# Neighbour sums of a two-layer GNN: four tiles of a slot in one burst, one-hots two slots ahead, and a gather ring that borrows the place of weights

## Chip, cores and metric

The kernel runs on one core of a Trainium2 chip. The metric is the device time of one execution in microseconds, as the median of several runs. A profile is one further execution, recorded by the hardware profiler.

## What is computed

The input `x` has 6250 nodes of 512 values, and there are 100,000 edges `src -> dst`, sorted by `dst`. Two mean-aggregating graph layers run on the normalised nodes, their result is added to `x`, and a mixture of eight experts with the best two per node is added to that.

```python
def _sage_layer(h, src, dst, W_self, W_neigh, b, n_nodes):
    agg = segment_sum(h[src], dst)
    deg = segment_sum(ones_like(dst), dst)
    h_neigh = agg / maximum(deg, 1.0)[:, None]
    return relu(h @ W_self + h_neigh @ W_neigh + b)
...
def _moe_forward(x, Wg, W1, b1, W2, b2, gamma, beta):
    topv, topi = top_k(xf @ Wg, 2)
    gate_w = softmax(topv)
    h = relu(einsum('td,edh->teh', xf, W1) + b1)
    y = layernorm(einsum('teh,ehd->ted', h, W2) + b2) * gamma + beta
    return sum(gate_w * take_along_axis(y, topi))
...
x = x + two _sage_layers(layernorm(x))
x = x + _moe_forward(layernorm(x))
```

All arithmetic on the rows is in float32.

## The kernel before

**Blocks, tiles, slots.** The nodes are cut into NB = 49 blocks of 128. The edges are cut into 782 tiles of 128. The row of each edge's source node is fetched from HBM by an indirect DMA that POOL issues (`gather`, L214), one per tile: 128 rows of 2 KB. A group is NQ x TS = 12 tiles, worked in TS = 3 slots of NQ = 4 tiles, so there are about 196 slots in a layer. For each slot DVE builds a one-hot table `hot` (`build`, L224), which says to which of 32 consecutive nodes an edge belongs. PE multiplies it with the gathered rows (`add`, L244): four tiles go to four column strips of 32 of PE's array and to the four quarters of one PSUM bank, `pa`. A matmul of float32 appears as two passes in the trace. After three slots `close` copies `pa` to SBUF (ACT, L252). When the groups that can hold a block's edges are closed, `prepare` builds selection matrices `sel` (DVE, L269), and `take_out` adds the strips up for the block (PE, L278). That happens every third slot, or, for 16 of the blocks, after six.

**What runs in the slots.** `sums` is called once for each layer. It writes the program of PE, DVE, ACT and POOL by hand, in the order of its loop. Within slot `i` the order was: `gather(i + ahead)`, then `build(i + 1)`, the sums of tiles 0 and 1, whatever is due in the place "mid", the sums of tiles 2 and 3, `close`, and whatever is due in the place "post". An engine executes its instructions in that order. The instructions of SP's queue are ordered by the compiler's scheduler.

What is due comes from `finish`, called by `take_out`:

- First layer (`layer1`): transposes u1 in "mid" two slots later, copied out of PSUM by ACT (L190), and the projection u2 on them in "post" of the same slot (L386); transposes u3 and projection u4 in the slot after; u5 in the next. For blocks from 19 on, u0 is one more projection.
- Second layer (`route`): DVE and ACT make the block's own result and its normalised rows `xn` (L833 to L839); then `turn` (transposes, "mid", slot 2), `logits` ("post", slot 2), `experts` ("mid", 3: a small transpose, then DVE chooses two experts), `rank` ("mid", 4: two small matmuls, then DVE counts places), `send` ("mid", 5 and 6: an indirect DMA of POOL scatters the rows to `xs`, L823) and `share` ("post", 6).
- Also in the second layer, from the time when the first lists of rows are known, `each` begins in every even slot the first expert product of one 128-row tile (an "up"): its rows are fetched by SP (L698), transposed by `turn_x` in "mid" three slots later, multiplied with W1 in `times` ("post" of that slot, L709), and turned by `turn_h` one slot later (L717, L720). These products are kept in HBM (`hd`).

After the second layer a last stage computes the remaining ups, the down products with W2 (L969), and the combination.

**Buffers.** The gathered rows of the first layer lie in 16 tiles, `rows_t`, of 256 KB, fetched three slots ahead. Those of the second layer lie in a ring of 12 such places in the tile `big`, behind W1, fetched two slots ahead (`ring`). W2 lies in the tile `w2`, 8 MB, loaded by SP with one DMA of 1 MB for each expert (`load_w2`, L455), asked for in `route` of blocks 1, 7, 13 and so on to 43. In SP's compiled order all eight stand at the start of the second layer. `xn` has two places, for even and odd blocks. `apart` is a memset of one element on POOL (L535), issued ahead of the scatters of the last four blocks.

Of the kernel before, what the change touches and what calls it, by code (L numbers as in the profile page):

```python
# [67 lines left out]
def gnn_moe(ctx, tc, x, src, dst, Ws1, Wn1, gb1, Ws2, Wn2, gb2, Wg, W1, b1, W2, b2, gamma, beta, out):  # L68
# [122 lines left out]
        return tT  # L191


    def sums(z, pool, pap, room, pn, finish, ring, nring, each=None):

        nslot = (NG - 1) * TS + min(TS, NT_E - (NG - 1) * NQ * TS)  # L200
        ahead = nring // NQ - 1
        tiles = [[t for t in range(i // TS * NQ * TS + i % TS, min(NT_E, (i // TS + 1) * NQ * TS), TS)]
                 for i in range(nslot)]
        gathered, hots, few, strips, counts, sels, due = {}, {}, {}, {}, {}, {}, {}
# [5 lines left out]
        def gather(i):  # L210
            if i < nslot:
                for t in tiles[i]:
                    gathered[t] = ring()
                    nc.gpsimd.indirect_dma_start(  # L214
                        out=gathered[t], out_offset=None, in_=z[:, :],
                        in_offset=bass.IndirectOffsetOnAxis(ap=srcT[:, t : t + 1], axis=0))
# [17 lines left out]
                nc.vector.tensor_add(few[g][:, :m], before[:, :m], hots[i][:, :m])  # L234
                few[g, j] = few[g]

        def add(i, qs):
            g, j = divmod(i, TS)
            if pa[0] is None:
                pa[0] = pap.tile([P, D], F32, name="pa", bufs=2)  # L240
            for q in qs:
                if q < len(tiles[i]):
                    t = tiles[i][q]
                    nc.tensor.matmul(pa[0][q * SW : (q + 1) * SW], hots[i][:, q], gathered.pop(t), start=(j == 0),  # L244
                                     stop=(j == TS - 1 or t == NT_E - 1), tile_position=(0, q * SW))

        def close(i):

# [32 lines left out]
            for behind, place, what in finish(b, ps) if pn is None else finish(b, ps, pn[:, 1]):  # L281
                at(i + behind, place, what)

        for i in range(ahead):
            gather(i)
        build(0)
        i = 0
        while i < nslot or any(k[0] >= i for k in due):
            gather(i + ahead)
            if each is not None:  # L290
                for behind, place, what in each(i):
                    at(i + behind, place, what)
            build(i + 1)
            if i < nslot:
                add(i, (0, 1))
            for what in due.pop((i, "mid"), ()):
                what()
            if i < nslot:
                add(i, (2, 3))
                if i % TS == TS - 1 or i == nslot - 1:  # L300
                    close(i)
            for what in due.pop((i, "post"), ()):
                what()
            i += 1
# [7 lines left out]
    def part(i):  # L312
        return big[:, i * D : (i + 1) * D]
# [61 lines left out]
    with tc.tile_pool(name="s1", bufs=2, side="right") as pool, \  # L375
            tc.tile_pool(name="s1a", bufs=1, space=PSUM) as pap, \
            tc.tile_pool(name="s1p", bufs=2, space=PSUM) as psp:

        def layer1(b, pa, pd):
            n = rows[b]  # L380
            r = slice(b * P, b * P + n)
            own = {}

            def project(ph, tT, w, start, stop):
                for c in range(C):
                    nc.tensor.matmul(ph, tT[:, c], w[:, c], start=(start and c == 0), stop=(stop and c == C - 1))  # L386

            def u0():
                ps = psp.tile([P, D], F32, name="pm")
                project(ps, xnT[b], ws1, True, True)  # L390
                nc.vector.tensor_add(part(b), ps, bb1)

            def u1():
                own["aT"] = transposed(pool, psp, own["a"], AF.Copy)

            def u2():
                ph = psp.tile([P, D], F32, name="pm")
                project(ph, own["aT"], wn1, True, True)
                own["h"] = pool.tile([P, D], F32, name="h")
                nc.vector.tensor_add(own["h"], ph, part(b))  # L400

            def u3():
                own["hT"] = transposed(pool, psp, own["h"], AF.Relu)

            def u4():
                pz = psp.tile([P, D], F32, name="pm")
                project(pz, own["hT"], wn2, True, True)
                t = pool.tile([P, D], F32, name="z")
                nc.scalar.copy(t, pz)
                nc.sync.dma_start(z2[r], t[:n])  # L410

            def u5():
                ps = psp.tile([P, D], F32, name="pm")
                project(ps, own["hT"], ws2, True, True)
                t = pool.tile([P, D], F32, name="s")
                nc.vector.tensor_add(t, ps, bb2)  # L416
                nc.sync.dma_start(s2[r], t[:n])

            nc.vector.tensor_copy(deg[:, b : b + 1], pd[:, 0:1])  # L419
            nc.vector.tensor_scalar(rcnt[:, b : b + 1], deg[:, b : b + 1], 1.0, None, op0=OP.max)  # L420
            nc.vector.reciprocal(rcnt[:, b : b + 1], rcnt[:, b : b + 1])
            own["a"] = pool.tile([P, D], F32, name="a")
            nc.scalar.activation(own["a"], pa, AF.Copy, scale=rcnt[:, b : b + 1])
            e = (b - 5) // 4
            if b >= 5 and (b - 5) % 4 == 0 and e < NE:

                nc.sync.dma_start(w1[:, e * KD : (e + 1) * KD].rearrange("p (c h) -> p c h", c=C),
                                  W1[e].rearrange("(c p) h -> p c h", p=P))
            return ([] if b < NS else [(1, "post", u0)]) + [(2, "mid", u1), (2, "post", u2), (3, "mid", u3), (3, "post", u4), (4, "post", u5)]

        with tc.manual_schedule(engines=HAND):
            sums(xn_d, pool, pap, lambda: pap.tile([P, D], F32, name="ps"),
                 pap.tile([P, 2, NDEG], F32, name="pn"), layer1,
                 lambda: pool.tile([P, D], F32, name="rows_t", bufs=16), 16)
    b_ctx.close()


# [298 lines left out]
    with tc.tile_pool(name="s2", bufs=2, side="right") as pool, \  # L736
# [3 lines left out]
        own = {}  # L740
        ready = {}
        at_slot = [0]
        nring = [0]

        bet = part(NW + 16)[:NE]
        nc.sync.dma_start(bet, beta)

        def ring():
            nring[0] += 1
            return part(NW + (nring[0] - 1) % 12)  # L750

        def fetch_own(b):
            if b < NB:
# [7 lines left out]
        def route(b, pa):  # L761
# [56 lines left out]
                nc.sync.dma_start(accs[r], acc[:n])  # L818

            def send(k):  # L820
                if b >= NB - 4:
                    apart()
                inst = nc.gpsimd.indirect_dma_start(  # L823
                    out=xs[:, :], out_offset=bass.IndirectOffsetOnAxis(ap=slot[:n, b, k : k + 1], axis=0),
                    in_=t["xn"][:n], in_offset=None)
                free_of(inst, "xs")
# [5 lines left out]

            nc.vector.scalar_tensor_tensor(a[:n], pa[:n], rcnt[:n, b : b + 1], a[:n], op0=OP.mult, op1=OP.add)  # L833
            nc.vector.scalar_tensor_tensor(acc[:n], a[:n], 0.0, acc[:n], op0=OP.max, op1=OP.add)
            if b % 6 == 1 and b // 6 < NE:
                load_w2(b // 6)
            mv, rs = norm_stats(pool, acc[:n], n)
            t["xn"] = part(NW + 13 + b % 2)
            nc.vector.tensor_scalar(t["xn"][:n], acc[:n], mv[:n, 0:1], rs[:n], op0=OP.subtract, op1=OP.mult)  # L839
# [20 lines left out]

        fetch_own(0)
        with tc.manual_schedule(engines=HAND):
            sums(z2, pool, pap, lambda: psp.tile([P, D], F32, name="ph"), None, route, ring, 12, each)
    g_ctx.close()


# [331 lines left out]
```

## Time and profile before

| | |
|---|---|
| median of 3 runs | 3282.5 us (3280.71 to 3284.29) |
| the profiled execution | 3665.66 us |
| its span | 3663.9 us |
| mean granted PE clock in it | 0.903 |
| PE busy | 3038.6 us, 83% |
| POOL busy | 1800.4 us, 49% |
| DVE busy | 1131.4 us, 31% |
| ACT busy | 659.3 us, 18% |
| moved by DMA | 698.76 MB, mean 191 GB/s |
| first sums | about 195 to 1480 us of the span |
| second sums | about 1490 to 2960 us, with ups from about 2000 |
| last stage | from about 2960 us |

A line of the timeline gives the start and the duration in us, the engine, the line of the kernel, the operation, what it writes and reads, and in brackets how long the engine was idle before and what ended that. In the groups, the numbers behind the bar are busy time, mean time of one in ns, and the idle time ahead of them with what ended it. "issue" is time in which the engine waited for nothing that the profile shows. "remote" and "another core or an unknown queue" name a release that the profile can't assign. A DMA of POOL has the time of its issue, not of its transfer.

### The profile page before, as it was taken

What the parts mean: (1) busy time and instruction counts of PE and PEld (TensorE: products, weight loads), DVE (VectorE), ACT (ScalarE), POOL (GpSimd) and SP (SyncE); (2) the same over time, 40 slices, a digit from 0 to 9 for tenths busy, and PEclk for the clock granted to TensorE, in tenths of its full rate; (3) what the DMA queues carried; (4) which work ended last, traced back from release to release, by engine and by line L of the source; (5) the groups of instructions that cost most, each with busy time, mean ns of one, the idle gap of its engine ahead of it and who ended that gap; (6) DMA issues with size and microseconds to landing.
All of it is one profiled execution on the core that took longest, in us unless ns stands there. A gap on an engine that the chain in (4) does not pass through costs nothing.

```text
span 3663.9 us, 33902 instructions
## 1 busy us (share of the span) xinstructions
PE 3038.6 (83%) x9794; PEld 1156.2 (32%) x9794; DVE 1131.4 (31%) x4001; ACT 659.3 (18%) x1188; POOL 1800.4 (49%) x1970
## 2 busy tenths in 40 slices
PE   7778888999999999466666888888888877999994
PEld 3223333333333333111111333333333333334442
DVE  5311111111111111132233333433343334443464
ACT  1211111111111111011111222222222211222221
POOL 0266555555555552466666555555555438000253
PEclk9889999999999999777777888898898988999997
DMA  6566666665666653666666766666677634441496
GB/s 241 183 186 203 199 195 200 192 185 177 185 188 176 178 171 103 239 200 208 199 204 200 214 214 215 209 217 213 214 228 218 189 105 155 135 132 61 156 308 233
DMA packets 269498, 698.76 MB, mean 191 GB/s; under 512 B 42448, under 2 KB 44090, under 8 KB 269148
## 3 DMA queue, kind: packets, MB, share of 16 engines
q0 software_dynamic: 142912, 463.42, 42.9%
q1 hardware_dynamic: 121372, 224.59, 17.9%
q10 hardware_dynamic: 5024, 8.50, 0.7%
q8 instruction: 85, 1.39, 0.2%
q14 instruction: 105, 0.86, 0.1%
HBM read 557.43 MB, written 139.71 MB: 190 GB/s over the span
## 4 chain that ended last, share of the span: by engine, by line
PE 70%; another core or an unknown queue 10%; DVE 7%; issue 6%; DMA 4%; ACT 2%; SPq 0%; DVEq 0%; POOL 0%; ACTq 0%; POOLq 0%
PE pm L386 17%; PE pa L244 15%; PE py L969 9%; PE ph L709 7%; PE ph L278 5%; PE pt L188 4%; PE ph L945 3%; PE ps L278 2%; PE ph L816 2%; PE pm L366 2%; DMA out<-acc 1%; PE small L775 1%; DMA xt<-in_x 1%; PE pt L717 1%
## 5 line engine op out<-in xcount | busy, mean ns | idle before, releaser
L214 POOL DMA_INDIRECT rows_t<-xn_d,srcT x782 | 742.1, 949 | 654.9 <-PE pa L244 262.9
L214 POOL DMA_INDIRECT big<-z,srcT x782 | 752.6, 962 | 609.3 <-issue 167.9
L244 PE MATMUL pa<-big,hot 128*32 128x512 f32 x1564 | 443.9, 684 | 107.5 <-DVE hot L224 63.0
L969 PE MATMUL py<-w,hT 128*128 x840 | 395.4, 614 | 40.4 <-DVE y L986 21.8
L244 PE MATMUL pa<-rows_t,hot 128*32 128x512 f32 x1564 | 348.5, 632 | 93.1 <-DVE hot L224 30.0
L386 PE MATMUL pm<-wn,tT 128*128 128x512 f32 x784 | 368.6, 613 | 22.0 <-ACT tT L190 21.7
L709 PE MATMUL ph<-big,xgT 128*128 x544 | 288.7, 680 | 68.7 <-ACT xgT L190 24.0
L905 POOL DMA_INDIRECT big<-ys,yrow x98 | 107.4, 1096 | 427.6 <-DMA ys<-y 331.3
L969 PEld LDWEIGHTS py<-w,hT 128*128 128x128 f32 x840 | 153.6, 193 | 219.3 <-issue 172.1
L386 PEld LDWEIGHTS pm<-wn,tT 128*128 128x128 f32 x784 | 144.9, 195 | 207.8 <-issue 163.7
L709 PEld LDWEIGHTS ph<-big,xgT 128*128 128x128 f32 x544 | 113.2, 219 | 230.5 <-issue 143.9
L386 PE MATMUL pm<-ws,tT 128*128 128x512 f32 x392 | 181.1, 605 | 0.0
L190 ACT ACTIVATE tT<-pt 128x512 f32<-128x512 f32 x117 | 69.0, 596 | 565.4 <-PE pt L188 408.7
L244 PEld LDWEIGHTS pa<-big,hot 128*32 128x32 f32 x1564 | 65.9, 114 | 247.9 <-issue 111.7
L945 PE MATMUL ph<-big,xgT 128*128 x296 | 136.9, 605 | 0.0
L823 POOL DMA_INDIRECT xs<-big,slot x98 | 98.8, 1008 | 71.6 <-DVE g L560 44.0
L419 DVE COPY deg<-pn 128x1 f32<-128x1 f32 x49 | 7.7, 158 | 408.4 <-PE pn L280 245.2
L720 DVE TENSOR_SCALAR hT<-pt,b1T 128x128 f32<-128x128 f32 x272 | 76.6, 344 | 166.4 <-PE pt L717 132.3
L976 DVE BATCH_NORM_STATS2 st<-py 128x6 f32<-128x512 f32 x105 | 73.2, 697 | 160.2 <-PE py L971 157.8
L244 PEld LDWEIGHTS pa<-rows_t,hot 128*32 128x32 f32 x1564 | 47.4, 110 | 233.5 <-issue 130.8
L416 DVE TENSOR_TENSOR s<-pm,bb 128x512 f32<-128x512 f32 x49 | 33.9, 691 | 272.0 <-PE pm L386 272.0
L224 DVE TENSOR_TENSOR hot<-rel,iota_row 128x128 f32<-128x128 bf16 (+1 forms) x394 | 106.0, 281 | 26.6 <-issue 12.4
(622 smaller groups left out, 3391.5 us busy)
## 6 DMA issues: line engine op xcount, KB each, us to landing
xg<-xs SPq DMA_DIRECT2D x105, 256.0 KB
ys<-y SPq DMA_DIRECT2D x105, 256.0 KB
hd<-hT SPq DMA_DIRECT2D x68, 256.0 KB
hT<-hd SPq DMA_DIRECT2D x68, 256.0 KB
rows_t<-xn_d,srcT POOLq DMA_INDIRECT x782
big<-z,srcT POOLq DMA_INDIRECT x782
xt<-in_x SPq DMA_DIRECT2D x12, 1024.0 KB
xn_d<-xn SPq DMA_DIRECT2D x12, 1024.0 KB
```

The source lines that it names most:

```text
L188: nc.tensor.transpose(pt[:, c, :n], t[:n, c * P : (c + 1) * P], ident[:n, :n])
L214: nc.gpsimd.indirect_dma_start(out=gathered[t], out_offset=None, in_=z[:, :], in_offset=bass.IndirectOffsetOnAxis(ap=srcT[:, t : t + 1], a ...
L224: nc.vector.tensor_tensor(hots[i][:, :m], rel.rearrange("p (c j) -> p j c", j=TS)[:, j, g * NQ : g * NQ + m] .rearrange("p (t o) -> p t o" ...
L244: nc.tensor.matmul(pa[0][q * SW : (q + 1) * SW], hots[i][:, q], gathered.pop(t), start=(j == 0), stop=(j == TS - 1 or t == NT_E - 1), tile ...
L278: nc.tensor.matmul(ps, sel[:k], st[:k], start=(g == a), stop=(g == z))
L386: nc.tensor.matmul(ph, tT[:, c], w[:, c], start=(start and c == 0), stop=(stop and c == C - 1))
L709: nc.tensor.matmul(ph, self.xT[:, c], w1[:, bass.ds(self.e * KD + c * D, D)], start=(c == 0), stop=(c == C - 1))
L720: nc.vector.tensor_scalar(hT[:, c], pt[:, c], b1T[:, bass.ds(self.e * HC + c, 1)], 0.0, op0=OP.add, op1=OP.max)
L823: inst = nc.gpsimd.indirect_dma_start(out=xs[:, :], out_offset=bass.IndirectOffsetOnAxis(ap=slot[:n, b, k : k + 1], axis=0), in_=t["xn"][: ...
L905: nc.gpsimd.indirect_dma_start(out=yk[:n], out_offset=None, in_=ys[: ready[0] * P, :], in_offset=bass.IndirectOffsetOnAxis(ap=yrow[:n, b, ...
L945: nc.tensor.matmul(ph, u.xT[:, c], w1[:, bass.ds(u.e * KD + c * D, D)], start=(c == 0), stop=(c == C - 1))
L969: nc.tensor.matmul(py, hT[:, c], w2[:, bass.ds(e * KD + c * D, D)], start=(c == 0), stop=False)
```

## The change

1. `add` sums all four tiles of a slot in one burst. What was due in "mid", between the halves, comes after the burst.
2. `build` runs two slots ahead in place of one.
3. The number of slots that a gather runs ahead becomes a function, `ahead`. In the first layer it stays 3. In the second layer `ring` has seven groups of four places for the slots before `near` = 147: three in `big` as before, and four in the half of `w2` that belongs to experts 4 to 7. The gathers then run six slots ahead. From slot 147 on it is three groups and two slots as before.
4. The loads of W2 for experts 4 to 7 are asked for in `route` of blocks 40, 42, 44 and 46. In SP's compiled order they stand behind the load of the input rows of about block 36.
5. `apart` is issued ahead of each of the 98 scatters, in place of the last eight.

```diff
@@ -191,14 +191,13 @@
         return tT
-    def sums(z, pool, pap, room, pn, finish, ring, nring, each=None):
+    def sums(z, pool, pap, room, pn, finish, ring, ahead, each=None):
-        ahead = nring // NQ - 1
         tiles = [[t for t in range(i // TS * NQ * TS + i % TS, min(NT_E, (i // TS + 1) * NQ * TS), TS)]
                  for i in range(nslot)]
         gathered, hots, few, strips, counts, sels, due = {}, {}, {}, {}, {}, {}, {}
@@ -210,7 +209,7 @@
         def gather(i):
             if i < nslot:
                 for t in tiles[i]:
-                    gathered[t] = ring()
+                    gathered[t] = ring(i, t)
                     nc.gpsimd.indirect_dma_start(
                         out=gathered[t], out_offset=None, in_=z[:, :],
                         in_offset=bass.IndirectOffsetOnAxis(ap=srcT[:, t : t + 1], axis=0))
@@ -234,15 +233,13 @@
                 nc.vector.tensor_add(few[g][:, :m], before[:, :m], hots[i][:, :m])
                 few[g, j] = few[g]
-        def add(i, qs):
+        def add(i):
             g, j = divmod(i, TS)
             if pa[0] is None:
                 pa[0] = pap.tile([P, D], F32, name="pa", bufs=2)
-            for q in qs:
-                if q < len(tiles[i]):
-                    t = tiles[i][q]
-                    nc.tensor.matmul(pa[0][q * SW : (q + 1) * SW], hots[i][:, q], gathered.pop(t), start=(j == 0),
-                                     stop=(j == TS - 1 or t == NT_E - 1), tile_position=(0, q * SW))
+            for q, t in enumerate(tiles[i]):
+                nc.tensor.matmul(pa[0][q * SW : (q + 1) * SW], hots[i][:, q], gathered.pop(t), start=(j == 0),
+                                 stop=(j == TS - 1 or t == NT_E - 1), tile_position=(0, q * SW))
         def close(i):
@@ -281,22 +278,23 @@
             for behind, place, what in finish(b, ps) if pn is None else finish(b, ps, pn[:, 1]):
                 at(i + behind, place, what)
-        for i in range(ahead):
-            gather(i)
+        asked = 0
         build(0)
+        build(1)
         i = 0
         while i < nslot or any(k[0] >= i for k in due):
-            gather(i + ahead)
+            while asked < nslot and asked - ahead(asked) <= i:
+                gather(asked)
+                asked += 1
             if each is not None:
                 for behind, place, what in each(i):
                     at(i + behind, place, what)
-            build(i + 1)
+            build(i + 2)
             if i < nslot:
-                add(i, (0, 1))
+                add(i)
             for what in due.pop((i, "mid"), ()):
                 what()
             if i < nslot:
-                add(i, (2, 3))
                 if i % TS == TS - 1 or i == nslot - 1:
                     close(i)
             for what in due.pop((i, "post"), ()):
@@ -431,7 +429,7 @@
         with tc.manual_schedule(engines=HAND):
             sums(xn_d, pool, pap, lambda: pap.tile([P, D], F32, name="ps"),
                  pap.tile([P, 2, NDEG], F32, name="pn"), layer1,
-                 lambda: pool.tile([P, D], F32, name="rows_t", bufs=16), 16)
+                 lambda i, t: pool.tile([P, D], F32, name="rows_t", bufs=16), lambda i: 3)
     b_ctx.close()
@@ -740,14 +738,21 @@
         own = {}
         ready = {}
         at_slot = [0]
-        nring = [0]
+
+
+        FAR = 7
+        near = (NG - 1) * TS * 11 // 14 // FAR * FAR
         bet = part(NW + 16)[:NE]
         nc.sync.dma_start(bet, beta)
-        def ring():
-            nring[0] += 1
-            return part(NW + (nring[0] - 1) % 12)
+        def ring(i, t):
+            q = t // TS % NQ
+            k = i % FAR if i < near else (i - near) % 3
+            return part(NW + k * NQ + q) if k < 3 else w2[:, (16 + (k - 3) * NQ + q) * D : (17 + (k - 3) * NQ + q) * D]
+
+        def ahead(i):
+            return FAR - 1 if i < near else 2
         def fetch_own(b):
             if b < NB:
@@ -818,8 +823,7 @@
                 nc.sync.dma_start(accs[r], acc[:n])
             def send(k):
-                if b >= NB - 4:
-                    apart()
+                apart()
                 inst = nc.gpsimd.indirect_dma_start(
                     out=xs[:, :], out_offset=bass.IndirectOffsetOnAxis(ap=slot[:n, b, k : k + 1], axis=0),
                     in_=t["xn"][:n], in_offset=None)
@@ -832,8 +836,11 @@
             nc.vector.scalar_tensor_tensor(a[:n], pa[:n], rcnt[:n, b : b + 1], a[:n], op0=OP.mult, op1=OP.add)
             nc.vector.scalar_tensor_tensor(acc[:n], a[:n], 0.0, acc[:n], op0=OP.max, op1=OP.add)
-            if b % 6 == 1 and b // 6 < NE:
+            if b % 6 == 1 and b // 6 < NE // 2:
                 load_w2(b // 6)
+            e = NE // 2 + (b - NB + 9) // 2
+            if b >= NB - 9 and (b - NB) % 2 and e < NE:
+                load_w2(e)
             mv, rs = norm_stats(pool, acc[:n], n)
             t["xn"] = part(NW + 13 + b % 2)
             nc.vector.tensor_scalar(t["xn"][:n], acc[:n], mv[:n, 0:1], rs[:n], op0=OP.subtract, op1=OP.mult)
@@ -860,7 +867,7 @@
         fetch_own(0)
         with tc.manual_schedule(engines=HAND):
-            sums(z2, pool, pap, lambda: psp.tile([P, D], F32, name="ph"), None, route, ring, 12, each)
+            sums(z2, pool, pap, lambda: psp.tile([P, D], F32, name="ph"), None, route, ring, ahead, each)
     g_ctx.close()
```

## Prediction

> **What bounds the kernel now.** I read the table of stages first, since the page's shares are means over stages with different limits.
>
> ```profile
> 200.00:1420.00 1220.00, 1123.78 (x3829) 426.60 (x3829) 218.22 (x779) 150.65 (x248) 704.77 (x743) 0.96 0.63 187
> 1560.00:2000.00 440.00, 276.40 (x897) 77.90 (x897) 132.80 (x572) 75.27 (x129) 282.77 (x294) 0.75 0.68 204
> 2000.00:2900.00 900.00, 749.92 (x2602) 277.33 (x2602) 329.80 (x1397) 214.12 (x369) 514.21 (x533) 0.89 0.69 215
> ```
>
> The columns are the stretch, then busy time of PE, weight loads, DVE, ACT and POOL, then granted clock, DMA share and GB/s. First sums (200 to 1420): PE is 92% busy at clock 0.96, so PE is the limit. Second sums without expert work (1560 to 2000): PE 63% at clock 0.75. A gather occupies POOL for 0.96 us plus a 0.30 us gap (timeline), so 294 POOL instructions take about 294 x 1.26 = 370 of 440 us: POOL is nearly the limit. Second sums with the ups (2000 to 2900): PE 83%, POOL 533 x 1.26 = 672 of 900. Here PE and the short waits on its chain decide. After 3100 PE is at 100% in the slices, and the change touches nothing there.
>
> Next, the timeline of PE and ACT in a steady piece of the first sums:
>
> ```profile
> 410.26 1.07 PE L244 MATMUL pa<-rows_t,hot 128*32 128x512 f32 x8
> 411.26 3.70 PE L386 MATMUL pm<-ws,tT 128*128 128x512 f32 x8
> 414.89 1.05 PE L244 MATMUL pa<-rows_t,hot 128*32 128x512 f32 x4
> 415.87 0.66 PE L188 MATMUL pt<-ident,a 128*128 128x128 f32 x4
> 416.46 1.05 PE L244 MATMUL pa<-rows_t,hot 128*32 128x512 f32 x4
> 417.44 0.18 PE L256 MATMUL pn<-ones_h,few 128*128 128x8 bf16 x1
> ...
> 416.63 0.60 ACT L190 ACTIVATE tT<-pt 128x512 f32<-128x512 f32 x1 [4.93 <-PE pa L244]
> ```
>
> The reader is to see three things. Four tiles at once (x8, two passes each) take 1.00 us to the next instruction, and two tiles (x4) take 0.98: a split slot pays the sum twice. Transposes stand between the halves. And the second half runs while ACT copies the transposes out, which the next matmul (L386 at 417.48) needs: the second half is mostly cover for ACT.
>
> Then the waits and POOL:
>
> ```profile
> PE pa L244 <- DVE hot L224: 13.0, 11, 1.7
> ...
> L214 POOL DMA_INDIRECT big<-z,srcT x262 | 251.9, 962 | 147.8 <-issue 53.9 <-remote 34.1 <-PE small L794 26.3
> L823 POOL DMA_INDIRECT xs<-big,slot x32 | 31.6, 989 | 9.7 <-issue 8.8 <-DMA big<-z,srcT 0.6 <-DVE g L560 0.3
> ...
> 1510.79 1.00 POOL L214 DMA_INDIRECT big<-z,srcT  x1 [11.27 <-PE pa L244]
> ...
> 2890.06 0.09 POOL L535 MEMSET tick<- 1x1 f32 x1
> 2890.37 0.99 POOL L823 DMA_INDIRECT xs<-big,slot  x1 [0.22 <-issue]
> ```
>
> In neither stretch of the second sums does a landing gather stand among PE's long waits. The only such waits, 6.2 us in 3, are at the start, 1420 to 1560. So the deeper ring takes no large PE wait away.
>
> The profiled execution took 3665.7 us, its span 3663.9, and the median of the runs is 3282.5: 383 us apart. The chain puts 9.9% (363 us) on "another core or an unknown queue", stops in which several engines rest together. I take these for what sets the profiled execution apart; in the runs shown POOL's and PE's own work then fills more of the time.
>
> [...]
>
> **The change, part by part.**
>
> 1. *Halves joined, first sums.* Each of 49 blocks has two split slots (transposes u1, u3): 98. Removed: a 0.98 us half. Late next: ACT's copy. The transposes end at 416.53, ACT starts 0.10 later, takes 0.60, and PE follows some 0.05 behind (as at 2319.28 after ACT's end at 2319.23). L386 can then start at 417.28, not 417.48: 0.20 won. In the u3 slot at 402 it is 0.16. 98 x 0.18 = **18 us**. Bounds: 0, and 98 x 0.98 = 96 if ACT's copy were hidden elsewhere.
>
> 2. *Halves joined, second sums.* A block's slots after its take-out are turn (2), experts (3) and rank (4). Turn, like an up's turn_x, is followed by matmuls on ACT's copy: 0.18 again. Experts and rank feed nothing in their slot: the full 0.98. In the stretch without ups (17 blocks) POOL hides it: 0 (up to 34 x 0.98 = 33 if it doesn't). With ups, 32 blocks remain, and a turn_x falls in every odd slot. Half of the 64 experts and rank slots are even: 32 x 0.98 = 31. 16 turns lie beside a turn_x, where the second transposes cover ACT's first copy: 16 x 0.8 = 13. The other 16 turns and some 48 odd slots: 64 x 0.18 = 11. Sum **55 us**.
>
> 3. *One-hots built two slots ahead.* In the stretch with ups PE waits 13.0 us for `hot`, queued on DVE behind route's work (L833 to L839). That goes; late next is `xn` (L839), which the transposes need, about 0.2 us behind. **10 us** with ups. Without them 38.1 us of such waits lie under POOL's pace: 0, at most 38. In the first sums PE waits for `hot` at the stops, where ACT's copy of `a` comes next: 0. DVE has the same instructions, and is 37% busy at most in these stretches.
>
> 4. *Ring of 28 in place of 12.* At the start POOL issues 12 gathers, then waits 11.27 us for PE. With 28 places it goes on, and since POOL is nearly the limit up to 2000, I count **10 us** (0 to 11). After that POOL reaches a place only when its old tile is summed, as now. In its queue four more groups of gathers stand ahead of each scatter: when POOL is behind, scatters come later, and the `xn` they free (two buffers) holds up DVE L839 and then PE's turn. Ups' fetches on SP wait for scatters too (141.7 us of SP waits with ups). Neither binds while PE trails POOL, which the longer ring lets it do: 0, bound +15. From slot 147 on the ring is three groups again, as now.
>
> 5. *Late W2 loads.* Eight 1 MB loads are issued from 1488 to 1513, in DMA at full share (359, 374 and 387 GB/s in three slices of 10 us). Four move behind the row load of about block 36 in SP's compiled order, when their places are free, so SP and the fetches behind don't wait for PE. At the start 4 MB less, some 11 us of transfer, but POOL issues without a gap from 1510.79 to 1544: 0, at most 11. Later 4 MB meet gathers two slots ahead: **+3** (0 to +10). They are to be complete for the down matmuls near 3000.
>
> 6. *90 more memsets on POOL.* The one at 2890.06 takes 0.09 us inside the usual gap, and the scatter starts 0.31 after the DMA before, as without: 0. If the gap ran beside it: 90 x 0.09 = +8.
>
> Sum: -18 - 55 - 10 - 10 + 3 = **-90 us**. On the profiled execution that is 3576, a ratio of 0.975, which gives 3202 for the median; taken off directly, 3192. Between them: **3197 us**. My own bounds: from -35 (10 and 30 for parts 1 and 2, 5 each for 3 and 4, +15 of delays) to -150 (30, 80, 25, 15), so 3132 to 3247.
>
> **Rivals.**
>
> *POOL holds all of the second sums.* In the runs the stops are gone, and 782 x 1.26 + 98 x 1.29 = 1112 us of POOL stand against a stage of 1400 in the profile. Parts 2 and 3 are then hidden, and 18 + 10 remain: **3254**. For it: 383 us must have gone somewhere, mostly here. Against: PE is 83% busy with ups.
>
> *The deep ring pays.* POOL's idle time in 1560 to 2000 is 157.5 us, of which 294 x 0.30 = 88 is gap. If the other 69 come back as prefetch, beside the 90: **3123**. For: PE's pace is uneven, with ups in every second slot. Against: no PE wait for gathers there.
>
> *Slower: the clock.* The halves removed kept PE busy while it waited. If busy share falls and the granted clock with it, as from 0.89 (83% busy) to 0.75 (63%), the rest of the work stretches. From 0.89 to 0.82 with ups costs 750 x 0.085 = 64 us, from 0.96 to 0.93 in the first sums 1124 x 0.032 = 36, and 10 more at the start: 110 against 90, so **3302**. It decides once the clock with ups falls below about 0.83 and the first sums lose as much. Against: the added waits are 0.7 us, and no stretch here shows a clock that fell for waits so short.
>
> *It does nothing:* the cover is all of it, and the delays of parts 4 and 5 eat the rest: 3282.
>
> **Numbers.** My forecast 0.57, deep ring 0.16, POOL 0.14, clock 0.09, nothing 0.04. About 0.2% (6.6 us) can be told from no change. Faster 0.87, same 0.04, slower 0.09. The range from 3115 to 3265 leaves out the clock, nothing, and some of the deep ring's tail.
>
> **What would show it.** Right: `pa` only in x8 groups, L386 about 0.75 us after the transposes' end with short waits on ACT `tT`, `hot` gone from PE's waits, POOL without the 11 us gap at the start, rank and experts slots 1 us shorter, the memset inside the gap. Wrong: a granted clock below 0.83 with ups; PE waiting long for `xn` or `xg`; gathers waited for after slot 147; or a POOL idle time much below 69 us before 2000.

## The result and the profile after

| | before | after |
|---|---|---|
| median of 4 runs, us | 3283.39 (3280.71 to 3287.09) | 3240.39 (3234.37 to 3252.99) |
| ratio | | 0.9873, 95% interval 0.9838 to 0.9908 |
| profiled execution, its span, us | 3665.66, 3663.9 | 3235.02, 3233.2 |

The change made the kernel 43 us faster, where 85 were forecast. Executions of either kernel come with stops of about 11 us (the kernel before then takes about 3655 us) or without (about 3280), alike for a whole session; the profile shown ahead of the prediction has stops, the profile after has none, so the stages are compared here with a later profile of the kernel before without stops (run g3_before, 3283.88 us, span 3282.1).

The table of stages shows the stretch, then busy time of PE, weight loads, DVE, ACT and POOL, then granted PE clock, DMA share and GB/s. The stretches run from the first to the last `pa` sum of the first layer, then over the first 74 slots of the second, then over the rest. Before, without stops:

```profile
152.87:1303.62 1150.75, 1145.11 (x3957) 430.66 (x3957) 224.43 (x802) 153.99 (x253) 739.31 (x779) 1.00 0.68 207
1370.13:1778.57 408.44, 311.21 (x983) 80.73 (x983) 137.37 (x580) 78.87 (x137) 308.82 (x321) 0.88 0.79 250
1778.57:2531.57 753.00, 702.27 (x2683) 261.33 (x2684) 342.75 (x1455) 218.18 (x377) 525.17 (x549) 0.98 0.81 265
```

And after:

```profile
151.32:1290.45 1139.13, 1062.71 (x3957) 421.32 (x3957) 223.42 (x802) 148.85 (x253) 739.94 (x779) 1.00 0.70 210
1360.02:1756.49 396.47, 245.43 (x983) 76.76 (x987) 133.83 (x574) 78.08 (x136) 303.63 (x344) 0.79 0.79 242
1756.49:2485.93 729.44, 623.33 (x2688) 254.77 (x2680) 342.56 (x1460) 214.40 (x378) 528.07 (x607) 0.95 0.86 279
```

Three things are to be seen. PE is busy 82, 66 and 79 us less in the three stages, but these are only 11.6, 12.0 and 23.6 us shorter: most of the work removed came back as idle time. In the first sums PE's clock stays at 1.00; in the last stretch it falls from 0.98 to 0.95. And before the ups (1360 to 1756 after) POOL's issues fill the stage: at 1.26 us for a gather and 1.29 for a scatter they make 405 of 408 us before and 397 of 396 after. With the ups they leave 66 of 753 us free before and 45 of 729 after.

The two profiled executions lie 48.9 us apart and the medians 43, and the runs of the changed kernel spread over 19 us. Shares of the gain that are read from one profile of each kernel, as below, are good to a few microseconds only.

The timeline of PE in a slot with u3, then the copy on ACT:

```profile
858.01 1.06 PE L241 MATMUL pa<-rows_t,hot 128*32 128x512 f32 x8
859.01 0.66 PE L188 MATMUL pt<-ident,h 128*128 128x128 f32 x4
860.41 3.70 PE L384 MATMUL pm<-wn,tT 128*128 128x512 f32 x8 [0.75 <-ACT tT L190]
```

```profile
859.76 0.60 ACT L190 ACTIVATE tT<-pt 128x512 f32<-128x512 f32 x1 [4.96 <-PE pt L188]
```

The form is the one forecast: one x8 group, transposes, and 0.75 us of waiting for ACT. Over the first sums that is one line of PE's waits (total us, times, longest):

```profile
PE pm L384 <- ACT tT L190: 70.8, 95, 1.0
```

At the start of the second sums POOL's waits hold what was forecast too. Before, then after:

```profile
POOL big L214 <- PE pa L244: 15.2, 14, 11.2
```

```profile
POOL big L213 <- PE pa L241: 2.7, 9, 0.3
```

The wait of 11.2 us is gone. And the memset costs nothing, since its 0.09 us lie in the usual gap of 0.30 us ahead of the scatter:

```profile
2099.20 0.95 POOL L213 DMA_INDIRECT big<-z,srcT  x1 [0.30 <-PE small L786]
2100.14 0.09 POOL L533 MEMSET tick<- 1x1 f32 x1
2100.45 0.99 POOL L827 DMA_INDIRECT xs<-big,slot  x1 [0.22 <-issue]
```

### The profile page after: what moved, and what is told of

The parts are those of the page before. It is cut to its first block, busy times and chain, and to the rows that moved or that the text cites. A ratio compares the mean times of both kernels' runs of the same rounds, so it can differ in the third digit from the quotient of the medians.

```text
span 3233.2 us, 33788 instructions
## 1 busy us (share of the span) xinstructions
PE 2716.4 (84%) x9794; PEld 1101.1 (34%) x9794; DVE 1128.7 (35%) x4001; ACT 647.5 (20%) x1188; POOL 1807.1 (56%) x2060
## 4 chain that ended last, share of the span: by engine, by line
PE 66%; DMA 17%; DVE 6%; ACT 3%; issue 3%; POOL 3%; SPq 0%; DVEq 0%; ACTq 0%; POOLq 0%
PE pm L384 19%; PE py L976 10%; PE pa L241 9%; PE ph L707 7%; PE ps L275 4%; DMA w<-z,srcT 4%; DMA big<-z,srcT 3%; PE pt L188 3%; PE ph L952 3%; PE ph L275 2%; ACT tT L190 2%; PE pm L364 2%; DMA rows_t<-xn_d,srcT 2%; DMA out<-acc 1%; DMA xs<-big,slot 1%
## 5 line engine op out<-in xcount | busy, mean ns | idle before, releaser
L213 POOL DMA_INDIRECT big<-z,srcT x446 | 427.8, 959 | 216.3 <-issue 77.7
L213 POOL DMA_INDIRECT w<-z,srcT x336 | 322.9, 961 | 104.5 <-issue 61.8
L707 PE MATMUL ph<-big,xgT 128*128 x544 | 271.4, 645 | 54.7 <-ACT xgT L190 51.5
L241 PE MATMUL pa<-rows_t,hot 128*32 128x512 f32 x1564 | 240.4, 607 | 18.9 <-DMA rows_t<-xn_d,srcT 17.8
L707 PEld LDWEIGHTS ph<-big,xgT 128*128 128x128 f32 x544 | 105.0, 203 | 186.9 <-issue 114.5
L241 PE MATMUL pa<-big,hot 128*32 128x512 f32 x892 | 152.0, 632 | 11.7 <-DMA big<-z,srcT 10.8
L188 PE MATMUL pt<-ident,big 128*128 128x128 f32 (+1 forms) x196 | 35.5, 309 | 122.7 <-DVE big L846 111.6
L952 PE MATMUL ph<-big,xgT 128*128 x296 | 136.9, 605 | 0.0
L241 PE MATMUL pa<-w,hot 128*32 128x512 f32 x672 | 116.4, 663 | 4.5 <-DMA w<-z,srcT 4.2
```

Source lines behind the costliest of these rows:

```text
L188: nc.tensor.transpose(pt[:, c, :n], t[:n, c * P : (c + 1) * P], ident[:n, :n])
L213: nc.gpsimd.indirect_dma_start(out=gathered[t], out_offset=None, in_=z[:, :], in_offset=bass.IndirectOffsetOnAxis(ap=srcT[:, t : t + 1], a ...
L707: nc.tensor.matmul(ph, self.xT[:, c], w1[:, bass.ds(self.e * KD + c * D, D)], start=(c == 0), stop=(c == C - 1))
L952: nc.tensor.matmul(ph, u.xT[:, c], w1[:, bass.ds(u.e * KD + c * D, D)], start=(c == 0), stop=(c == C - 1))
```

## The experiments

Theory: what PE saved in sums came back, since the second halves had covered waits (for ACT, DVE and POOL) and kept PE's clock up. Rivals: the burst meets its gathers too late; POOL alone holds the second sums.

### Taking the change apart, without stops

**g4_halves and g3_before.** The changed kernel with the two halves back (ring, late loads, memsets and one-hots two ahead stay), beside the kernel before.

```diff
-                add(i)
+                add(i, (0, 1))
             for what in due.pop((i, "mid"), ()):
                 what()
             if i < nslot:
+                add(i, (2, 3))
```

> The changed kernel with the halves put back (the deeper ring, late second weights and one-hots two ahead stay). Without stops: if the burst is all of the gain, 3283 (ratio 1.00); by the prediction's sum the rest gives 17 of 90, so 0.995. With stops 3649, ratio 0.9986, as in the first look.

> The kernel before, once more, for a profile of it in the same session. If the session has no stops it takes 3283, and its stages can be set against those of the changed kernel: I expect first sums about 1157 us, second sums about 1185. If it has stops: 3655, and it tells nothing new.

g3_before took 3283.88 us, with first sums of 1151 us and second sums of 1161. g4_halves took 3256.96 us, ratio 0.9932 (0.9915 to 0.9948). Its stages:

```profile
151.34:1302.04 1150.70, 1144.64 (x3956) 431.15 (x3957) 223.46 (x802) 153.99 (x253) 739.45 (x779) 1.00 0.68 207
1371.91:1769.95 398.04, 255.11 (x983) 76.66 (x984) 134.49 (x574) 78.89 (x136) 304.56 (x346) 0.82 0.77 242
1769.95:2509.13 739.18, 694.25 (x2688) 259.36 (x2682) 342.25 (x1460) 218.72 (x378) 526.24 (x605) 0.99 0.83 275
```

Set between the two others this shares out the gain. Ring and one-hots: 0 in the first sums, 10.4 and 13.8 us in the second. The burst: 11.6, 1.6 and 9.7 us. So the forecast's 55 us for halves joined in the second sums became 11.

Where the rest went is read in the last stretch, halves against burst. The groups of PE give busy time and mean ns behind the bar. With halves:

```profile
L710 PE MATMUL ph<-big,xgT 128*128 x480 | 220.4, 602 | 17.7 <-ACT xgT L190 16.1 <-DVE hot L223 1.3
L243 PE MATMUL pa<-big,hot 128*32 128x512 f32 x628 | 162.8, 604 | 0.0
L243 PE MATMUL pa<-w,hot 128*32 128x512 f32 x348 | 89.4, 609 | 0.0
```

With the burst:

```profile
L707 PE MATMUL ph<-big,xgT 128*128 x480 | 238.4, 643 | 51.7 <-ACT xgT L190 48.5 <-issue 2.1 <-DVE hot L223 1.0
L241 PE MATMUL pa<-big,hot 128*32 128x512 f32 x628 | 93.5, 604 | 3.1 <-DMA big<-z,srcT 3.1
L241 PE MATMUL pa<-w,hot 128*32 128x512 f32 x348 | 49.3, 617 | 0.0
```

The sums fell by 252.2 - 142.8 = 109.4 us. The same 480 matmuls of the ups took 18.0 us more, 643 ns in place of 602, and the take-outs (L275, 198 of them) 11.1 more: 29 us lost to a lower clock. PE's idle time rose from 44.9 to 106.1 us, by 61.2. 109 less 29 and 61 leaves 19; the stage shows 9.7. Busy times of groups overlap at their ends, so all groups add up to 73 us more than PE's busy time with halves (767.5 against 694.3) and to 65 us more with the burst (688.1 against 623.3): 8 of the 9 us. The largest of the waits, with halves and then with the burst:

```profile
PE ph L710 <- ACT xgT L190: 16.1, 18, 1.8
PE ph L277 <- DVE sel L268: 7.8, 3, 6.3
```

```profile
PE ph L707 <- ACT xgT L190: 48.5, 36, 4.8
PE ph L275 <- DVE sel L266: 18.8, 12, 5.8
PE small L814 <- DVE gates L560: 8.8, 11, 1.8
```

With halves the wait for `gates` is not there. None of these is a wait for a gather; those are 3.1 us in 3. That speaks against the rival of late gathers in executions without stops. And as POOL has 45 us free here, its issues alone don't set the length of this stretch.

How the clock fell is seen in short windows. In these stretches it changes only on a grid of 3.41 us, and in each window of the grid it is either 1.00 or 0.50. Here are three windows in a row of the changed kernel, around a take-out that waited 1.06 us for `sel`:

```profile
1938.71:1942.12 3.41, 2.35 (x14) 0.82 (x8) 2.26 (x15) 2.57 (x4) 2.80 (x4) 1.00 0.75 198
1942.12:1945.53 3.41, 3.41 (x4) 1.45 (x5) 1.79 (x6) 0.24 (x1) 2.64 (x4) 0.50 0.92 339
1945.53:1948.95 3.42, 2.72 (x17) 0.81 (x15) 2.19 (x4) 0.00 (x0) 2.51 (x4) 1.00 0.93 277
```

PE was busy for 2.35 us of the first window (69%), and the second ran at half clock. In the whole stretch 22 of 213 windows ran so, with halves 4 of 216; 18 windows more at half speed are 31 us, which fits the 29. In both profiles every fall came after a window with PE busy for at most 72%. Of such windows at full clock there are 42 with the burst (18 were followed by a fall) and 11 with halves (2 were).

**g1_fill.** Filler in the place of the second half, in the first sums.

```diff
             for what in due.pop((i, "mid"), ()):
                 what()
             if i < nslot:
+                if spare is not None and len(tiles[i]) == NQ:
+                    for q in (2, 3):
+                        nc.tensor.matmul(spare[0][q * SW : (q + 1) * SW], hots[i][:, q], spare[1], start=True, stop=True, ...
```

> The changed kernel with filler: in the first sums, where the second half of a group's sums stood before, PE gets two matmuls of the same form (128x32 by 128x496) on a resident tile, into an unused part of the degree bank. They wait for no gather. It adds some 98 x 0.98 = 96 us of PE work and computes nothing. Theory 'PE's rest' (the burst costs time because PE stands 0.75 us in each slot and its clock is granted lower): where the profile has stops, first sums are about as fast as with halves there (3672, ratio 1.004, against 1.018 for the change itself). Rival 'gathers' (the burst needs the last two gathers of a slot some 4.7 us earlier, and so is hit by each late one): filler does not help, ratio 1.018 or more. In executions without stops PE's rest would give a ratio of 0.995 to 1.00, since filler takes back the 20 us that the burst saved there.

It took 3324.98 us, ratio 1.0139 (1.0119 to 1.0159). The expectation counted 98 slots, but the filler stands in all 195 full ones, so the total misses. The first sums:

```profile
151.26:1375.55 1224.29, 1221.17 (x4736) 455.84 (x4737) 224.65 (x802) 148.89 (x253) 738.87 (x779) 1.00 0.65 195
```

PE is busy to within 3 us of the stage, and the 76 us of idle time of the changed kernel are filled. But the clock was 1.00 with those pauses and is 1.00 without: in the first sums, without stops, the theory's clock half is wrong. The waits are the whole cost there. A pause of 0.75 us leaves PE busy for 78% of a 3.41 us window, and in the first sums of the changed kernel PE was busy for 77% or more in all but one of 331 such windows.

### A version with real work as cover

**g2_behind and i2_behind.** The burst goes behind the transposes, so that it covers ACT's copy itself. In slots of u3 it stays ahead, since it covers DVE's `h` there; u0 of the next block moves between u3 and u4 and covers the copy.

```diff
+            mid = due.pop((i, "mid"), ())
+            front = pn is not None and len(mid) and mid[-1].__name__ == "u3"
+            if i < nslot and front:
+                add(i)
-            for what in due.pop((i, "mid"), ()):
+            for what in mid:
                 what()
+            if i < nslot and not front:
+                add(i)
...
-            return ([] if b < NS else [(1, "post", u0)]) + [(2, "mid", u1), (2, "post", u2), (3, "mid", u3), (3, "post", u4), ...
+            return [(2, "mid", u1), (2, "post", u2), (3, "mid", u3)] + ([] if ... else [(3, "post", lambda: u0(b + 1))]) + [(3, "post", u4), ...
```

> The changed kernel with the covers put back out of real work: the burst stands behind the transposes (covers ACT's copy with its own 1.00 us), except in the slots of u3, where it stays ahead (it covers DVE's h) and the self projection u0 of the next block (3.7 us) moves between the transposes and u4. Theory 'PE's rest': both copies are hidden, the 0.75 us wait in each slot goes; without stops 98 x 0.75 = 73 us less in the first sums, as far as POOL allows (some 60), and up to 20 in the second sums: ratio about 0.965; with stops about 0.98. Rival 'gathers': the later burst is also easier to feed, so the same sign, but PE's waits for ACT's tT then stay or turn into waits for rows_t. Rival 'POOL holds': without stops no more than 0.98, with POOL at over 95% by its 1.26 us for a gather.

> The kernel with the burst behind the transposes, once more. Without stops 0.9707, as before. With stops the theory 'cover and clock' says that it loses none of what the burst loses there (1.018): ratio 0.985 to 1.00, so not slower than halves (0.9986). Rival 'the gathers are late for a burst': slower than the halves there, 1.005 or more.

3178.23 us, ratio 0.9707 (0.9687 to 0.9726), and in another session 3179.15 us, 0.9695 (0.9681 to 0.9709): faster than both kernels, where there are no stops. It was not run with stops, so what it does there is open. A slot of u3 in PE's timeline, and then the stages:

```profile
858.71 0.66 PE L188 MATMUL pt<-ident,h 128*128 128x128 f32 x4
859.20 3.60 PE L388 MATMUL pm<-ws,big 128*128 128x512 f32 x8
862.63 3.60 PE L388 MATMUL pm<-wn,tT 128*128 128x512 f32 x8
```

```profile
150.65:1251.44 1100.79, 1058.85 (x3965) 423.81 (x3965) 223.65 (x803) 154.00 (x253) 738.54 (x779) 1.00 0.71 217
1316.61:1717.60 400.99, 231.01 (x987) 73.21 (x987) 137.64 (x583) 79.56 (x137) 306.95 (x348) 0.77 0.78 242
1717.60:2430.56 712.96, 612.86 (x2681) 256.79 (x2680) 339.87 (x1452) 215.88 (x377) 524.58 (x603) 0.95 0.85 284
```

No pause stands ahead of u4. The first sums gain 38 us more, where some 60 were expected; in their place waits for DVE's `h` come up, 24.3 us in 31. In the second sums only 12 more are won, and their sum is 1114 us. The issues that fall into these two stretches take POOL 1081 us of it: all 401 before the ups, and 680 of 713 with them. (The 1112 us of the prediction's rival count the whole layer, with the gathers issued ahead of the first sum.)

**i1_behind_relief.** The same, with a quarter of the second sums' gathers left out.

```diff
-                for t in tiles[i]:
+                for q, t in enumerate(tiles[i]):
+                    if pn is None and q == 3:
+                        gathered[t] = gathered[tiles[i][2]]
+                        continue
                     gathered[t] = ring(i, t)
```

> The kernel with the burst behind the transposes, with POOL relieved in the second sums as in the two runs before (the fourth tile of a slot is not gathered, the third is summed in its place: not the reference's sums). Theory 'cover and clock': with the covers back it beats the halves with relief, in the first sums by some 30 us and in the second by 10 to 40. With stops that is about 3345, a ratio of 0.917 (halves 0.932, burst 0.953). Rival 'POOL alone': once POOL is relieved it stands where burst and halves stand in the second sums (1156 to 1173 us), ratio about 0.925 to 0.935. Without stops: below 3178 by whatever POOL holds there; 3060 to 3120 if POOL holds the second sums of this version, 3150 or more if it does not.

3050.30 us, ratio 0.9298 (0.9284 to 0.9313), in the session of i2_behind. The second sums:

```profile
1319.74:1633.32 313.58, 195.46 (x986) 65.89 (x987) 136.50 (x583) 79.81 (x137) 239.79 (x276) 0.83 0.79 249
1633.32:2300.43 667.11, 592.49 (x2681) 250.88 (x2680) 338.02 (x1452) 215.66 (x377) 408.08 (x480) 0.98 0.78 255
```

With the same instructions on PE they are 133 us shorter, 87 before the ups and 46 with them, and the clock with ups is back at 0.98. So in this version the gathers hold the second sums. The run takes away POOL's issue and the bytes together; that it is the issue is argued from PE's short waits for gathers (3.4 us in 4 in the last stretch of g2_behind), not shown.

How POOL's pace reaches PE is seen in the changed kernel's waits from 1360 to 1756, DVE's and then PE's:

```profile
DVE big L846 <- DMA xs<-big,slot: 88.7, 11, 16.8
```

```profile
PE pt L188 <- DVE big L846: 102.8, 14, 18.4
```

DVE waits for scatters, which stand in POOL's queue behind gathers; they hold the two places of `xn` (L846), and PE's turn waits for `xn`. Before, DVE's wait was 23.3 us, and PE waited for `hot` (59.9 us) and gathers (33.1).

### With stops

The remaining runs fell in sessions with stops. Ratios are to the kernel before in the same session (3653 to 3656 us).

| run | ratio | 95% interval |
|---|---|---|
| e0_before, the kernel before again | 1.0003 | 0.9978 to 1.0027 |
| a1_after, the changed kernel | 1.0183 | 1.0149 to 1.0216 |
| e1_halves, as g4_halves | 0.9986 | 0.9968 to 1.0003 |
| e8_l1halves, halves in the first sums alone | 1.0042 | 1.0026 to 1.0059 |
| e2_hot1, burst and ring, `build(i + 1)` | 1.0149 | 1.0110 to 1.0188 |
| e3_ring12, burst and one-hots two ahead, 12 places | 1.0166 | 1.0137 to 1.0194 |
| e4_burst, the burst alone | 1.0145 | 1.0106 to 1.0183 |
| h4_burst, again | 1.0140 | 1.0113 to 1.0166 |
| e6_ring28, ring, late loads and memsets alone | 1.0016 | 0.9991 to 1.0041 |
| h3_ring28, again | 1.0033 | 1.0017 to 1.0050 |
| h1_burst_relief, changed kernel, fewer gathers | 0.9529 | 0.9503 to 0.9556 |
| h2_halves_relief, e1_halves, fewer gathers | 0.9324 | 0.9298 to 0.9350 |

The kernel before, run again as e0_before, was to tell whether the stops belong to one profiled execution alone (then about 3283 us) or come again (about 3660): it took 3658 us.

The edits are those above, and for e2 and e3 (e3 also has `ahead` at 2 and all eight loads of W2 early, as in the kernel before):

```diff
-            build(i + 2)
+            build(i + 1)
...
-            return part(NW + k * NQ + q) if k < 3 else w2[:, (16 + (k - 3) * NQ + q) * D : (17 + (k - 3) * NQ + q) * D]
+            return part(NW + i % 3 * NQ + q)
```

> The changed kernel itself beside the kernel before. If its runs are free of the stops in which all engines rest: 0.987 of before, as in the result. If both kernels have the stops here (before near 3650 us), and the bursts are what costs there, as the two kernels with bursts of the last runs suggest (1.015 and 1.017 of before): 1.00 to 1.02 of before, so the gain is gone.

> The changed kernel with the sums of a slot again in two halves around the mid work; ring and one-hots as changed. As the prediction had it, the burst brings 73 us, so this is about 3240 + 73 = 3313. If POOL sets the pace in the first 19 blocks of the first sums and in the second sums up to about block 18 or beyond, the burst is worth less: 15 in the first sums and 10 to 25 in the second, so 3265 to 3280.

> The changed kernel with halves in the first sums alone; bursts stay in the second. Prediction: the first sums' burst brings 18 us, so 18 slower than the changed kernel. If POOL holds the first 19 blocks: 10 to 12. If bursts lower the clock in the first sums (runs with stops): faster than the changed kernel by 20 to 40.

> The changed kernel with one-hots built one slot ahead again. Prediction's term: 10 us, so 3250. If POOL holds the second sums: within 5 us of 3240.

> The changed kernel with the ring of 12 places, gathers two slots ahead and all eight W2 loads early, as before; bursts and one-hots two ahead stay. Prediction: the ring brings 10 at the start and costs 3, so 3247. If the ring's late scatters hold up xn and cost more than the start brings: 3220 to 3235, faster than the changed kernel. If the ring carries the gain: 3265 or more.

> The kernel before with the bursts alone; ring of 12, one-hots one slot ahead. By the prediction's terms 73 us less than before, a ratio of 0.978. If POOL sets the pace in the first 19 blocks of the first sums and through most of the second sums: 20 to 40 us, 0.988 to 0.994. If the runs have the stops: 1.01 to 1.02.

> The kernel before with the burst alone. If its gain does not depend on the ring and the one-hots: 0.9873 against 0.9932, so 19 us of 3280, ratio 0.994. If POOL at 12 places holds the second sums, only the first sums' 12 us: 0.996. If the gathers are now late for a burst: 1.00 or above.

> The kernel before with the ring of 28 alone, its late W2 loads and the memsets; halves and one-hots one ahead stay. Prediction: 7 us less, 0.998. If POOL holds the second sums and the ring takes its idle time away: 11 at the start and up to 60 after, 0.98 to 0.99. If late scatters hold up xn for nothing: 1.002 to 1.005.

> The kernel before with the longer ring, the late second weights and the memsets alone. Together with one-hots two ahead they gave a ratio of 0.9932 in the session without stops. By the prediction's sum the ring and the late loads give 7 of these 22 us (0.998); if the ring does all of it, 0.993; if only the one-hots matter, 1.000.

Here the burst makes the kernel slower, alone as well as with the rest, and taking it out brings all of it back. Most of it is in the first sums: halves in those alone bring 1.0183 to 1.0042. First sums of e1_halves, then of a1_after:

```profile
151.46:1427.88 1276.42, 1169.88 (x3957) 440.10 (x3958) 222.94 (x802) 153.96 (x253) 740.11 (x779) 0.96 0.63 187
```

```profile
152.66:1468.93 1316.27, 1109.85 (x3957) 442.26 (x3957) 223.21 (x802) 148.84 (x253) 738.73 (x779) 0.94 0.61 181
```

PE is busy 60 us less and idle 100 us more. The clock falls from 0.96 to 0.94; without stops it stayed at 1.00 and idle time rose by 70. What the stops are was not settled, nor why a burst suffers from them more. Each session of these experiments ran on another chip (0, 4 and 7 with stops, 8 and 9 without), so chip and session can't be told apart. Ring and one-hots bring nothing there; the ring alone is level in one session and 0.3% slower in another. As no run of the ring alone fell in a session without stops, how the 24 us of the two divide stays open.

> The changed kernel, with POOL relieved in the second sums: the fourth tile of each slot is not gathered there, PE sums the third tile in its place again (so the sums are not the reference's). 196 gathers of 782 go, 196 x 1.26 = 247 us of POOL, and a quarter of the gathered bytes; PE's instructions are the same. Theory 'POOL holds the second sums': the stage falls from 1125 us to PE's own pace, 1000 to 1050, and here the burst is faster than the halves by 30 to 55 us. Rival 'cover and clock' (in the stage PE loses by longer waits and a lower clock what it saves in sums): the stage falls too where PE waited for POOL, but burst and halves stay within 15 us of each other.

> The same relief of POOL with the halves put back (so again not the reference's sums). Theory 'POOL holds the second sums': second sums 30 to 55 us longer than in the run with the burst, in all 40 to 65 with the first sums' 12. Rival 'cover and clock': in all 10 to 25 us.

The second sums of h1_burst_relief, then of h2_halves_relief:

```profile
1544.77:1936.60 391.83, 233.02 (x982) 76.08 (x986) 135.97 (x574) 78.65 (x136) 246.56 (x283) 0.72 0.67 205
1936.60:2717.41 780.81, 639.51 (x2688) 261.38 (x2680) 340.58 (x1460) 214.71 (x378) 406.54 (x472) 0.92 0.69 215
```

```profile
1495.86:1879.08 383.22, 258.47 (x983) 77.96 (x985) 136.18 (x574) 79.02 (x136) 243.95 (x282) 0.80 0.67 208
1879.08:2651.90 772.82, 711.68 (x2687) 266.21 (x2682) 342.52 (x1460) 218.79 (x378) 406.04 (x474) 0.97 0.69 219
```

With fewer gathers both are over 230 us shorter here (e1_halves: 484 + 915, a1_after: 486 + 918). But the burst is still not faster than the halves, 1173 us against 1156, with the clock at 0.92 against 0.97. Both expectations were of one theory against the other; the runs show both at once. The gathers hold the stage, and when they are relieved, cover and clock take what the burst saves. That pair was not run without stops, so this is shown only with them.

## Why the prediction was right in direction and half wrong in size

- **Stops and stages.** That stops set the profiled execution apart was right: without them first and second sums of the kernel before are 1151 and 1161 us. The sum was still made in stages with stops, where POOL seemed to have 70 us free before the ups (440 less 370) and 228 with them (900 less 672). Without stops it had 3 and 66.
- **Part 1, halves joined in the first sums: 18 forecast, 11.6 measured.** The mechanism was right, down to the 0.75 us wait. The gain is 0.12 us a slot in place of 0.18; in the slots looked at, from the start of the sums to the projection, it is 2.55 us to 2.40 with u3 and 2.59 to 2.39 with u1. Set side by side, the take-outs of g4_halves and of the changed kernel draw apart by 12.5 us over the last 40 of the 49 blocks, 0.16 a slot, so in the steady part the term is nearly right. Over the first eight blocks the changed kernel falls 0.9 us behind; why was not traced.
- **Part 2, halves joined in the second sums: 55 forecast, 11.3 measured. This step failed.** The count of sums was right: its 112 slots of 0.98 make 110 us with ups, and 109 went. The cover was under-priced by little: 55 in the sum, 61 us of idle time measured. The term that failed is the clock, put at nothing because single waits of 0.7 us seemed too short to lower it. In the short windows each fall came after 3.41 us with PE busy for at most 72%, a share in which such waits add up: 22 windows ran at half clock in place of 4, and the same matmuls took 29 us more. The 1.6 us without ups, where POOL holds, agree with the forecast's 0.
- **Parts 3 to 6: 17 forecast, 24 measured.** Before the ups, 10.4 us against the ring's 10, and POOL's first wait went. With ups 13.8 us for one-hots and ring against 10 less 3; the wait for `hot` there was 26.8 us in place of the 13.0 that were read. The late scatters of part 4 came as described. PE waited 102.8 us for `xn` before the ups, which the prediction had named as a sign of being wrong; it cost nothing that shows, as POOL sets the pace there. With ups such waits are 8.8 us in 2. The memsets are free.
- **The rivals.** *POOL holds all of the second sums* was the nearest in number, 3254 against 3240, but in part by luck. Before the ups it is right. With ups it left nothing to win, where 23.6 us were won and POOL still had 45 free, and it counted 18 for part 1. It comes closer to the truth in the version with the covers back, where POOL needs 1081 of 1114 us and leaving out a quarter of the gathers brings 133. *The clock* was set aside because no stretch showed a clock that fell for waits of 0.7 us. That holds in the first sums (1.00), but not with ups, where waits reach 5.8 us and the clock went from 0.99 to 0.95. It stayed well above the 0.83 at which that rival would have turned the change into a loss. *The deep ring pays* is wrong: without stops POOL had no idle time to give back before the ups, 321 DMAs by 1.26 us are 404 of 408.

## What to carry to other kernels

Before a stage's savings are added up, set them against the time that the stage's other engine needs just to issue its own instructions, counted within the stage: before the ups POOL left 3 of 408 us, and the burst brought 1.6. Instructions that look like waste between dependent steps may be cover: price their removal as the work saved, less the waits laid open, less the slower clock of the rest, from a profile of the kind of execution that is to be forecast. To see whether a slower clock threatens, look at PE's busy share in windows of a few microseconds (here 3.41 us, with every fall after a share of 72% or less): neither the mean of the stage (85% with the burst) nor the single wait showed it. A gain of 101 us, above the forecast, came without stops when the one burst and an independent projection were put where the waits had been.

## What the runs showed of the hardware

- In the stretch with ups of the changed kernel PE's granted clock was 1.00 or 0.50 in every window of a grid of 3.41 us. It fell 18 times, each time after a window with PE busy for 72% or less, and only two of these windows were wholly idle. 95 waits of about 0.75 us in the 1139 us of the first sums left it at 1.00 (it was 0.50 in their first 5.6 us alone, with PE busy throughout); there all but one of 331 windows were busy for 77% or more.
- One gather of 128 rows of 2 KB took POOL 0.96 us of issue and a gap of 0.30 us where nothing else held it up (its rows came later: the one begun at 1362.29 in the changed kernel held POOL for 0.95 us and landed 5.92 us after its start); before the ups these 1.26 us filled the stage in both kernels.
- The same kernel took 3280 us in some sessions and 3655 in others. In the second kind the first sums went from 1151 to 1289 us with the same instructions (run e0_before), and a change that is 1.3% faster in one kind was 1.8% slower in the other.
